# A graph-transformer block on one Trainium2 core: the ring of weights and the sums of their quarters move to the other side of on-chip memory

## The chip, the cores and the metric

The kernel runs on one core of one Trainium2 chip. The core has five engines that work at the same time, each through its own queue in order: TensorE (PE, the matmuls; its weight loads are listed apart as PEld), VectorE (DVE), ScalarE (ACT), GpSimd (POOL) and SyncE (SP), which here does nothing but issue DMA transfers. The metric is the device time of one launch in microseconds (us). Lower is better.

## The reference

The input x has 1250 nodes of 768 features; a graph of about 41,000 edges comes as two lists, src and dst. Cut to what matters here:

```python
xn = layernorm(x)
x = x + gnn(xn, edges) + mix(xn)
x = x + ffn(layernorm(x))

def gnn(xn, ...):            # two graph-attention layers: 4 heads, then 2 heads
    out1 = gat_conv(x_norm, src, dst, W1, ...)
    out2 = gat_conv(out1, src, dst, W2, ...)
    return concatenate([xn, out2]) @ Wu + bu

def mix(xn, ...):            # linear attention, 12 heads of 64
    q = elu(xn @ Wq + bq) + 1;  k = elu(xn @ Wk + bk) + 1;  v = xn @ Wv + bv
    kv = einsum(k, v);  z = 1 / einsum(q, k.sum())
    return (einsum(q, kv) * z) @ Wo + bo

def ffn(xl, ...):            # 8 experts of 384, the best 2 per node
    h = gelu(xl @ W1[e] + b1[e]);  y = h @ W2[e] + b2[e]
```

Everything is computed in 32-bit floats.

## The kernel before

The nodes are cut into ten tiles of 125 rows. The program has five stages, and each engine's instructions are put in order by a planner of the compiler, which lets later work go first where earlier work is blocked.

1. **Graph counts and features.** The edges become a 1250 x 1250 matrix of counts, `AT`, and a 0/1 matrix `mask`. The normalised, turned input stays in memory as `xnT`.
2. **Two layers of graph attention** (`attend`, lines 501 to 543). For each head ACT makes exponentials, DVE takes their maximum (line 541) and multiplies by the counts (line 542), and PE sums over neighbours (line 554 in the first layer, line 576 in the second).
3. **Keys and values** (lines 591 to 631). For each tile PE multiplies `xnT` by `Wk_sb` and `Wv_sb` (line 600). DVE makes keys of the one, ACT copies the other, PE multiplies them (line 614), and DVE adds the result to `kvacc` (line 620). The planner spreads these matmuls over the attention stage, where PE has time left; the last ones come after it. At the end DVE puts the bias of the values in and cuts the product to its heads (lines 628 and 630). Then PE turns `kvacc` (lines 673 and 674), and ACT copies it out as `kvT` and `ksum` (lines 675 and 676).
4. **Output of both branches.** `Wo_sb` is replaced by the product of `kvT` and `Wo` (lines 678 to 683: twelve matmuls of 384 columns, each of which the trace records as two). From then on queries, `Wo` and `Wu` are applied to pairs of tiles (`query(p)` and the loop from line 927). The big products, for Wq and for Wu, are done with seven products of quarters instead of eight (a scheme of Winograd's). For that, `quarters(W, T)` makes sums of the four quarters of a weight by four subtractions on DVE (lines 657 to 660): three results go to the tile T and one replaces a quarter of W. `pair(p)` makes the sums on the side of the input (lines 794 to 797). `product` is the matmul itself (line 802).
5. **Experts.** Nodes are gathered by expert with indirect DMAs on POOL (line 1029), turned, and put through the two layers of each expert (lines 1048 and 1060). The results are added to the output by indirect DMAs.

**Where tiles lie.** On-chip memory is handed out by pools stacked from two sides, left and right. Sizes below are bytes per partition. A pool that is opened after another was closed takes over its place, and the first instruction that writes there waits for the last one that used the old tile.

- On the left lie constants, then `xnT` (30,000; pool `big`), and in stages 1 to 3 the graph's tiles above it: `AT` 25,240, `mask` 12,500, `h2` 7,920 and `s1` 320. Above these come the attention's work tiles: `w` 3 x 5,000, `v` 2 x 5,000, `scr` 2,500, and the three rows `ss_row`, `up_row`, `dn_row` of 5,000 each. `graph.close()` (line 588) ends them after the second attention layer.
- On the right lie `kept` (31,680, holding among others `Wq_sb` and `kvT`), `kvacc` and its neighbours, and the pool `kp` of stage 3: `Wk_sb` 18,432, `Wv_sb` 18,432, `bk_b`, `ky`, `va` and `ke`, 50,712 in all. `kps.close()` (line 631) ends it.
- After that, the pool `mp` (`ksum`, `bq_b`) and the pool `wt` are opened on the right. `wt` is the ring of this case: four slots of 18,432 that hold in turn the sums of Wq's quarters (`aside[0]`), `Wo_sb`, `Wu_sb`, the sums of Wu's quarters (`aside[1]`), and later the weights of the experts, plus `Wu2_sb` (6,144) and `bu_b` (3,072). Behind them on the right lie the pool `fp` (expert biases, the gate's weights, `zero`, the broadcast biases `wb`) and, for stage 4 only, `rp` and `rl` (small tables and work tiles).
- `qp` (tiles `xt`, `qy`, `qe`, `qT` of stage 4) is opened on the left, above `xnT`. `first_half.close()` (line 1017) gives `xnT` up ahead of stage 5, and `sp`, the experts' work tiles, takes its place.

**Order of the DMA issues in the program** behind stage 3: `bq_b` (line 663), `Wo` and `Wu` (both by `load`, line 650), `Wu2_sb` (line 690), `fb`, `Wg_sb`, `bg_b` (lines 708 to 712), seven stores of zeros (lines 716 to 718), `bu_b` and `bo_b` (line 742), and then the tiles of x (line 933) and the weights of the experts (lines 699 to 704).

**What uses them.** `bq_b` is added to query products (line 819). `m1` and `w2` of lines 819 and 829 lie where `kvT` was, so they wait for line 682. `Wu2_sb` is read by the small product of line 748, whose result goes into `bu_b` (lines 743 and 750), which is added to every tile of x (line 934). `fb` is turned into `fb1T` (lines 774 and 775).

Of the kernel before, what the change touches and what calls it, by code (L numbers as in the profile page):

```python
# [27 lines left out]
F32 = mybir.dt.float32  # L28
# [10 lines left out]
N, D = 1250, 768  # L39
PT, NT = 125, 10  # L40
KC = D // 128
H1, C1, H2, C2 = 4, 192, 2, 96
# [27 lines left out]
def gps_block(ctx: ExitStack, tc: tile.TileContext, x, src, dst, norm_g, norm_b, W1, a_src1, a_dst1,  # L70
              b1, W2, a_src2, a_dst2, b2, Wu, bu, Wq, bq, Wk, bk, Wv, bv, Wo, bo, Wg, bg, fW1, fb1,
              fW2, fb2, out):
    nc = tc.nc
# [8 lines left out]
    const = ctx.enter_context(tc.tile_pool(name="const", bufs=1))  # L82
    small = ctx.enter_context(tc.tile_pool(name="small", bufs=3))
    dram = ctx.enter_context(tc.tile_pool(name="dram", bufs=1, space=bass.MemoryType.DRAM))
    first_half = ctx.enter_context(ExitStack())
    big = first_half.enter_context(tc.tile_pool(name="big", bufs=1))
    xr = x.rearrange("(t p) d -> p t d", p=PT)

    def token_rows(t):
# [550 lines left out]
    mp = ctx.enter_context(tc.tile_pool(name="mp", bufs=1, side="right"))  # L640
    ksum = mp.tile([PT, D], F32)
    bq_b = mp.tile([PT, D], F32)
    wt = ctx.enter_context(tc.tile_pool(name="wt", bufs=1, side="right"))
    q3 = KC // 2

    def weight():
# [31 lines left out]
    for c in range(KC):  # L678
# [7 lines left out]
    aside.append(weight())  # L686
    Ru = quarters(Wu_sb, aside[1].rearrange("p c f -> p (c f)")[:, :nt].rearrange(
        "p (c f) -> p c f", f=384))
    Wu2_sb = wt.tile([96, H2, D], F32)
    nc.sync.dma_start(Wu2_sb, Wu[D:].rearrange("(c p) f -> p c f", p=96))  # L690
    bu_b = wt.tile([PT, D], F32)


    fp = ctx.enter_context(tc.tile_pool(name="fp", bufs=1, side="right"))
# [32 lines left out]
    with ExitStack() as rs:  # L727
        rp = rs.enter_context(tc.tile_pool(name="rp", bufs=1, side="right"))
# [5 lines left out]
        def numbers(shape, pattern, base, mult, name, dt=F32):  # L734
# [2 lines left out]
                           allow_small_or_imprecise_dtypes=True)  # L737
            return t

        bo_b = qp.tile([PT, D], F32, name="xt")  # L740
        for t, a in ((bu_b, bu), (bo_b, bo)):
            nc.sync.dma_start(t, row_bcast(a, PT))
# [271 lines left out]


    mix.close()
    first_half.close()
    sp = ctx.enter_context(tc.tile_pool(name="sp", bufs=2))
    x_p = ctx.enter_context(tc.tile_pool(name="x_p", bufs=1, space=PSUM))
    h_p = ctx.enter_context(tc.tile_pool(name="h_p", bufs=2, space=PSUM))  # L1020
# [117 lines left out]
```

## Time and profile before

| | before |
|---|---|
| median of 3 runs | 1155.41 us (1152.61 to 1155.65) |
| the profiled execution, its own time | 1153.47 us |
| span of the profile | 1151.4 us |
| outside the span (1153.47 - 1151.4) | 2.07 us |
| PE busy | 1047.5 us (91%) |
| DVE busy | 706.8 us (61%) |
| ACT busy | 348.0 us (30%) |
| POOL busy | 74.3 us (6%) |
| mean granted PE clock | 0.973 of full speed |
| bytes moved by DMA | 79.76 MB, mean 69 GB/s |

The profile is one execution recorded by the hardware. Its views give the busy time of each engine, groups of instructions by line with what they waited for, the chain of work that ended last, and a timeline. Times within it count from the start of the span. A name such as `w` is the program's name for a tile with the number of its buffer left out: `w` with `in_L_mix_Wo_dram` is the ring's slot that receives Wo, and `kept` is the tile that holds `Wq_sb` and `kvT`. An ended wait is put down to the instruction whose signal came last. The granted clock is the share of PE's full clock that the chip let it have. PE's busy time counts modelled ends of matmuls, so it can hide waits of some tenths of a microsecond.

### The profile page before, as it was taken

What the parts mean: (1) busy time and instruction counts of PE and PEld (TensorE: products, weight loads), DVE (VectorE), ACT (ScalarE), POOL (GpSimd) and SP (SyncE); (2) the same over time, 40 slices, a digit from 0 to 9 for tenths busy, and PEclk for the clock granted to TensorE, in tenths of its full rate; (3) what the DMA queues carried; (4) which work ended last, traced back from release to release, by engine and by line L of the source; (5) the groups of instructions that cost most, each with busy time, mean ns of one, the idle gap of its engine ahead of it and who ended that gap; (6) DMA issues with size and microseconds to landing.
All of it is one profiled execution on the core that took longest, in us unless ns stands there. A gap on an engine that the chain in (4) does not pass through costs nothing.

```text
span 1151.4 us, 12014 instructions
## 1 busy us (share of the span) xinstructions
PE 1047.5 (91%) x4482; PEld 700.3 (61%) x4482; DVE 706.8 (61%) x1439; ACT 348.0 (30%) x522; POOL 74.3 (6%) x98
## 2 busy tenths in 40 slices
PE   2699998999999989988996999999999499999994
PEld 2596655579696969544553565666656356666653
DVE  7866667669696967769656757575755522222211
ACT  2141114464646454183832111111210011111111
POOL 1000000000000000000000000000000113222321
PEclk9999999999999999999997999999999689999997
DMA  5014000000000001100036001111144737787634
GB/s 160 28 46 173 14 28 1 1 1 1 1 1 1 1 0 44 40 1 1 14 83 217 9 28 54 41 41 41 41 141 136 241 80 190 216 208 213 124 56 57
DMA packets 35542, 79.76 MB, mean 69 GB/s; under 512 B 7006, under 2 KB 15536, under 8 KB 35468
## 3 DMA queue, kind: packets, MB, share of 16 engines
q1 hardware_dynamic: 29868, 59.06, 15.9%
q0 software_dynamic: 5600, 19.77, 8.5%
q8 instruction: 39, 0.64, 0.2%
q14 instruction: 35, 0.29, 0.1%
HBM read 60.48 MB, written 18.34 MB: 68 GB/s over the span
## 4 chain that ended last, share of the span: by engine, by line
PE 69%; DVE 21%; DMA 3%; issue 2%; ACT 2%; POOL 0%; DVEq 0%; POOLq 0%; ACTq 0%
PE s L802 18%; PE ph L1048 8%; PE mm L600 8%; PE py L1060 7%; PE mm L431 7%; DVE scr L521 6%; DVE w L541 5%; DVE w L542 5%; PE ag L554 3%; PE mm L861 2%; PE ag L576 2%; PE px L1032 2%; PE mm L406 2%; DMA out_dram<-ys,idx 1%; PE ec L351 1%
## 5 line engine op out<-in xcount | busy, mean ns | idle before, releaser
L554 PE MATMUL ag<-kept,w 125*125 125x198 f32 x800 | 137.4, 333 | 5.1 <-DVE w L542 4.9
L554 PEld LDWEIGHTS ag<-kept,w 125*125 125x125 f32 x800 | 133.5, 188 | 9.0 <-DVE w L542 9.0
L1048 PE MATMUL ph<-xsT,w 128*128 128x384 f32 (+1 forms) x324 | 100.7, 471 | 1.7 <-DVE xsT L1035 1.7
L1060 PE MATMUL py<-w,hT 128*128 128x384 f32 x300 | 100.6, 486 | 0.0
L431 PE MATMUL mm<-Wg,xnT 128*125 128x400 f32 x240 | 90.4, 514 | 1.1 <-DVE xnT L322 0.6
L541 DVE TENSOR_TENSOR w<-v,w 125x1250 f32<-125x1250 f32 x60 | 86.5, 1458 | 6.0 <-ACT w L539 5.3
L600 PE MATMUL mm<-Wv_sb,xnT 128*125 128x384 f32 x240 | 85.7, 489 | 4.8 <-DVE kvacc L620 4.8
L521 DVE CUSTOM_DVE_ANT_0 scr<-ss_row,mask 125x1250 bf16<-125x1250 f32 x60 | 87.5, 1459 | 0.5 <-ACT ss_row L512 0.2
L542 DVE SCALAR_TENSOR_TENSOR w<-w,AT 125x1250 f32<-125x1250 f32 x60 | 86.6, 1459 | 0.4
L1048 PEld LDWEIGHTS ph<-xsT,w 128*128 128x128 f32 x324 | 59.8, 194 | 41.3 <-DVE xsT L1035 2.3
L540 ACT ACTIVATE v<-dn_row,sl 125x1250 f32<-125x1250 f32 x60 | 79.4, 1335 | 17.3 <-DVE w L541 16.8
L600 PE MATMUL mm<-Wk_sb,xnT 128*125 128x384 f32 x240 | 84.4, 486 | 0.0
L802 PE MATMUL s<-w,qT 128*125 128x384 f32 x240 | 83.7, 490 | 0.0
L1035 DVE COPY xsT<-px 128x384 f32<-128x384 f32 x50 | 25.6, 553 | 86.7 <-PE px L1032 77.1
L1060 PEld LDWEIGHTS py<-w,hT 128*128 128x128 f32 x300 | 55.3, 190 | 33.9
L1063 DVE TENSOR_TENSOR ys<-py,wb 128x768 f32<-128x768 f32 x25 | 23.9, 958 | 72.4 <-PE py L1060 45.7
L600 PEld LDWEIGHTS mm<-Wv_sb,xnT 128*125 128x125 f32 x240 | 42.4, 187 | 31.1 <-DVE kvacc L620 7.0
L802 PE MATMUL s<-w 128*125 128x384 f32 x150 | 54.0, 494 | 7.5 <-DVE w L796 7.5
L802 PEld LDWEIGHTS s<-w,qT 128*125 128x125 f32 x240 | 43.3, 188 | 26.9 <-issue 0.2
L431 PEld LDWEIGHTS mm<-Wg,xnT 128*125 128x125 f32 x240 | 42.8, 191 | 26.8 <-issue 1.5
L539 ACT ACTIVATE w<-up_row,s 125x1250 f32<-125x1250 f32 x40 | 53.3, 1334 | 17.7 <-PE ag L554 17.5
L357 DVE TENSOR_TENSOR AT<-AT,ec 125x120 f32 x162 | 44.6, 275 | 19.9 <-PE ec L351 18.7
(296 smaller groups left out, 1458.8 us busy)
## 6 DMA issues: line engine op xcount, KB each, us to landing
w<-in_L_ffn_W_dram SPq DMA_DIRECT2D x18, 1152.0 KB
xt<-in_x_dram SPq DMA_DIRECT2D x20, 336.0 KB
wb<-in_L_ffn_b_dram SPq DMA_DIRECT2D x9, 384.0 KB
out_dram<-xt SPq DMA_DIRECT2D x10, 336.0 KB
xl_d<-xl SPq DMA_DIRECT2D x10, 336.0 KB
W_sb<-in_L_gnn_W_dram SPq DMA_DIRECT2D x1, 2304.0 KB
Wk_sb<-in_L_mix_Wk_dram SPq DMA_DIRECT2D x1, 2304.0 KB
Wv_sb<-in_L_mix_Wv_dram SPq DMA_DIRECT2D x1, 2304.0 KB
```

The costliest lines, as they stand in the source:

```text
L357: nc.vector.tensor_add(here, here, ec[:, g])
L431: nc.tensor.matmul(ps[:PT, :2 * (CG + 2)], xnT[:, c, t * PT:(t + 1) * PT], Wg1[:, c, 2 * k:2 * k + 2].rearrange("p h c -> p (h c)"), start ...
L521: nc.vector.tensor_tensor_reduce(scr, ss_row, mask[:, t], 1.0, 0.0, ALU.mult, ALU.max, top[:, t:t + 1])
L539: nc.scalar.activation(w, up_row, AF.Exp, bias=ss[:, st:st + 1])
L540: nc.scalar.activation(v, dn_row, AF.Exp, bias=sl[:, st:st + 1])
L541: nc.vector.tensor_tensor(w, v, w, op=ALU.max)
L542: nc.vector.scalar_tensor_tensor(w, w, 2.0, AT[:, st, :N], op0=ALU.min, op1=ALU.mult)
L554: nc.tensor.matmul(ag[:, t // 2, o:o + CG], w[:, t * PT:(t + 1) * PT], gw[:, st, hd], start=st == 0 and t % 2 == 0, stop=st == NT - 1, ski ...
L600: nc.tensor.matmul(ps[:PT, :384], xnT[:, c, t * PT:(t + 1) * PT], w[:, c, half], start=c == 0, stop=c == KC - 1)
L802: nc.tensor.matmul(ps, left[:, c], right[:, c], start=start and c == 0, stop=c == n - 1, skip_group_check=True)
L1048: nc.tensor.matmul(ph[:, :n * 128], w[0][:, o:o + 128], xT[:, c, :n * 128], start=c == 0, stop=c == KC - 1)
L1060: nc.tensor.matmul(py[:, k, :384], hT[:, f, j * 128:(j + 1) * 128], w[:, o:o + 384], start=f == 0, stop=f == FC - 1)
```

## The change

`wt` is opened on the left, above `xnT`, instead of on the right. It then covers 73,728 bytes that were the graph's 45,980, the attention's 27,500 of `w`, `v` and `scr`, and the first 248 of the row tiles. Since `qp` and later `sp` are stacked above `wt` on the left, `big` can't be closed ahead of stage 5 any more: it stays open to the end, and `first_half` goes. `Wu2_sb` and `bu_b` leave `wt` for `rp` on the right, and the load of `Wu2_sb` is written further down, behind the zeros and ahead of `bu_b`. With `wt` gone from the right, `fp`, `rp` and `rl` follow `mp` directly and lie where `kp` was.

```diff
-    first_half = ctx.enter_context(ExitStack())
-    big = first_half.enter_context(tc.tile_pool(name="big", bufs=1))
+    big = ctx.enter_context(tc.tile_pool(name="big", bufs=1))
...
     mp = ctx.enter_context(tc.tile_pool(name="mp", bufs=1, side="right"))
     ksum = mp.tile([PT, D], F32)
     bq_b = mp.tile([PT, D], F32)
-    wt = ctx.enter_context(tc.tile_pool(name="wt", bufs=1, side="right"))
+    wt = ctx.enter_context(tc.tile_pool(name="wt", bufs=1))
...
     Ru = quarters(Wu_sb, aside[1].rearrange("p c f -> p (c f)")[:, :nt].rearrange(
         "p (c f) -> p c f", f=384))
-    Wu2_sb = wt.tile([96, H2, D], F32)
-    nc.sync.dma_start(Wu2_sb, Wu[D:].rearrange("(c p) f -> p c f", p=96))
-    bu_b = wt.tile([PT, D], F32)
...
+        Wu2_sb = rp.tile([96, H2, D], F32)
+        nc.sync.dma_start(Wu2_sb, Wu[D:].rearrange("(c p) f -> p c f", p=96))
+        bu_b = rp.tile([PT, D], F32)
         bo_b = qp.tile([PT, D], F32, name="xt")
         for t, a in ((bu_b, bu), (bo_b, bo)):
             nc.sync.dma_start(t, row_bcast(a, PT))
...
     mix.close()
-    first_half.close()
     sp = ctx.enter_context(tc.tile_pool(name="sp", bufs=2))
```

No instruction that computes is added or removed.

## The prediction

> **What bounds the kernel now.** First the page's busy times and its 40 slices (28.8 us each).
>
> ```profile
> PE 1047.5 (91%) x4482; PEld 700.3 (61%) x4482; DVE 706.8 (61%) x1439; ACT 348.0 (30%) x522; POOL 74.3 (6%) x98
> ...
> PE   2699998999999989988996999999999499999994
> ...
> PEclk9999999999999999999997999999999689999997
> ```
>
> TensorE is the bound nearly everywhere. Behind the first stages it has two marked holes: slice 31 (a chain of small routing steps, which the change leaves alone) and around slice 21, where busy is 6 and the clock 7. The change touches the second. So I read it next, by stretches: length, then busy us of PE, PEld, DVE, ACT and POOL, granted clock, DMA share, GB/s.
>
> ```profile
> 589.30:594.20 4.90, 4.90 (x24) 2.97 (x23) 0.89 (x5) 1.77 (x4) 2.44 (x15) 1.00 0.55 158
> 594.20:602.20 8.00, 8.00 (x28) 4.48 (x26) 3.61 (x10) 0.52 (x1) 0.00 (x0) 1.00 0.78 195
> 602.20:605.50 3.30, 3.22 (x17) 2.25 (x17) 1.59 (x6) 1.08 (x6) 0.00 (x0) 1.00 0.04 15
> 605.50:609.00 3.50, 1.43 (x8) 0.96 (x8) 3.47 (x6) 2.12 (x12) 0.00 (x0) 1.00 0.38 92
> 609.00:617.66 8.66, 1.64 (x2) 0.49 (x3) 6.66 (x11) 0.00 (x0) 0.00 (x0) 0.57 1.00 372
> 617.66:625.00 7.34, 7.31 (x13) 3.70 (x14) 0.11 (x1) 2.51 (x6) 0.00 (x0) 0.58 0.85 294
> ```
>
> PE idles 2.07 us in the fourth line and 7.02 in the fifth, 9.09 together, and then works at little over half clock. The chain of work and SyncE's timeline say why.
>
> ```profile
> 594.42 7.74 PE mm L600 x24
> ...
> 603.87 0.57 DVE kvacc L620
> ...
> 606.22 11.33 DMA w<-in_L_mix_Wo_dram
> 617.69 11.62 PE mm L682 x24
> ```
>
> ```profile
> 568.51 0.35 SPq L625 DMA_DIRECT2D ky<-in_L_mix_bv_dram  x1
> 589.29 0.29 SPq L708 DMA_DIRECT2D fb<-in_L_ffn_b_dram  x1
> ...
> 605.89 0.28 SPq L663 DMA_DIRECT2D bq_b<-in_L_mix_bq_dram  x1
> 606.22 0.38 SPq L650 DMA_DIRECT2D w<-in_L_mix_Wo_dram  x1
> 606.64 0.54 SPq L650 DMA_DIRECT2D w<-in_L_gnn_Wu_dram  x1
> 607.23 5.32 SPq L690 DMA_DIRECT2D Wu_sb<-in_L_gnn_Wu_dram  x1
> ```
>
> Wo goes out only when stage 3 has ended, and the product of line 682 waits for it. SyncE's waits name both releasers:
>
> ```profile
> SPq L708 <- PE ag L576: 20.4, 1, 20.4
> SPq L663 <- DVE kvacc L628: 9.8, 1, 9.8
> ```
>
> `fb` now lies on the graph's ground and leaves as the last attention matmul ends, at 589.3. The loads on the ground of `kp` wait until 605.9. The planner passes later loads ahead of blocked earlier ones, as `fb` shows. The change swaps the two grounds.
>
> **The change part by part.**
>
> *Wo and Wu issue at about 589.4 instead of 606.2.* Wo's landing took 11.33 us beside Wu on the same queue, so Wo is there at 600.7. For both (4.72 MB): 1.5 us until bytes flow (the first full slice after the issue is 607 to 608), then 12.7 us at the 372 GB/s of the fifth line, so 603.6. The other end is the 195 GB/s of 594 to 602: 24.2 us, landing at 615.1. But that line holds small broadcast rows, which now go later; I take the first. What hides the loads: the last key and value matmuls, until 602.2.
>
> *The product of line 682* now waits for `kvT` instead. Its last copy in the trace ends at 608.45. So the product starts 9.2 us earlier at the latest (617.66 - 608.45).
>
> *The clock.* The product took 11.62 us; its last 12 records, at full clock, took 4.44 (624.78 to 629.22), so 24 take 8.9: 2.7 us gained. Line 802's pair in the fifth line took 1.64 where 0.81 is usual: 0.8 more. Here the Trainium skill ("TensorE: Matmul & The Clock Gate", The HAM clock gate) gives a smaller gain: half clock after about 3.4 us of idleness, full clock again after about 3.4 us of sustained work, so 1.7 us lost, a hole worth 9.09 + 1.7 = 10.8. The trace shows clock 0.50 from 611 to 623, 5 us and more after the product began: 3.5 lost, 12.6 in all. I use the trace. Against the change, the rule would charge again if the remaining gap reached 3.4 us; 605.5 to 609 has 2.07.
>
> *The remaining 2.07 us* end if PE has other work: the first query's quarter products 6, 7 and 2 (2.1 us each; four banks allow four until `m1`, which lies on `kvT`). They need the sums of Wq's quarters and of the input: 4 x 1.35 us and, for two pairs, 8 x 0.55 us on DVE, 9.8 us, now free to run from 589.3. DVE's idle time from 589.3 to 605.5 is 16.2 - 6.1 = 10.1 us, so they just fit. If that cover is gone they run behind `kvacc` as now and the gain is 12.6 - 2.07 = 10.5. I take 12.0, most of it filled.
>
> *What moves later.* `fb`, `Wg_sb`, `bg_b`, the zeros (589.29 to 593.93), `bo_b`, the first x tiles and `wb` now wait for `kp`. SyncE issues `bq_b` at 605.9, then 4.6 us of `fb` to zeros, then `Wu2_sb` at 610.9, `bu_b`, `bo_b` and x. With 3.6 us from issue to use (the x tile issued at 631.54, added at 635.13) `Wu2_sb` is there at 615. Its reader, line 748, follows the product, now ending at 617.4 (608.5 + 8.9): 2.4 us of slack. If the planner puts line 748 ahead of the product, PE stands until 615, 6.5 us. Line 774 (three transposes of `fb`, 0.23 us each) behind a landing at about 610: 0 to 2 us; I take nothing, since PE has queue entries with no such need. POOL's 15 small instructions (2.44 us) and DVE's two table steps serve routing at about 690; the slack is 80 us. `bq_b` needed 5.7 us from issue to line 668 beside Wo; its user, line 819, waits for the product anyway.
>
> *Edits at nothing.* `xnT` kept to the end, and `sp` on `qp`'s place: the first gather waits for `idx` (909.84 + 0.23), later than the last reader of `qT`; line 1012's last read of `rp`, under `sp`'s upper end, is at 911.8 against the gather's 911.06, so at most 0.7. The ring keeps four slots, so experts' loads keep their releases. From 640 to 880 PE idles 0.2 us; nothing there swallows a gain.
>
> **Sum.** 9.09 + 3.5 - 0.6 for imperfect filling = 12.0. Against the profiled execution: span 1151.4 - 12.0 = 1139.4, plus 2.07 outside = 1141.5. That execution (1153.47) lies 1.9 below the median of the runs, so against 1155.41 it is 1143.4. Changes under 0.3% (3.5 us) can't be told from none here.
>
> **Rivals.**
>
> *A new wait takes part of the place.* Line 748 ahead of the product (6.5), Wo and Wu at the slow rate (615.1 - 608.5 = 6.6), or DVE busy with new work when line 620 comes (one subtraction, 1.35). Gain 4 to 9; with 6.5 lost, 1149.9. For it: orders are the planner's, made from its own estimates. Against: 2.4 us of slack, and work to fill with.
>
> *The ring isn't free early.* Its 73,728 bytes take in 248 of the row tiles; were a tile of `kp` or anything living touched, or the release a joint one, Wo would go at 606.2 as now, `Wu2_sb` 4.6 us later than 607.2, and since its issue was held 5.3 us anyway, nothing moves: 1155.4. Against it: `fb`'s release at 589.3, and all those tiles belong to attention.
>
> *Slower: Wu's quarters block VectorE.* The four subtractions of line 657 to 660 on Wu (5.4 us) stood at 625 to 630.6, behind line 819. If the planner puts them ahead of line 620, everything behind, `kvacc`, `kvT`, the product, waits for Wu at L + 5.4 instead of 603.87, and PE goes cold (3.5). With L = 615.1 that costs 20.1: 1143.4 + 20.1 = 1163.5. It is worse than before by over 0.3% (15.5 lost) from L = 610.5 on. For it: Wu may now land while keys are unfinished. Against: L = 603.6 by the nearest row, and keys come first in the program.
>
> **How the numbers follow.** The full gain: 0.63, with its own range 1141 to 1146. A new wait: 0.18 (1146 to 1152). Not free: 0.07. Slower: 0.12. Faster by over 0.3% is the first two, 0.81; same 0.07; slower 0.12. The range leaves out the last two and little else: 1139.5 (all 12.6 of gain, 1142.8, and 3.3 for the scatter of the runs, which was 3.0) to 1152.5.
>
> **What would show it.** Right: Wo and Wu issued near 589.4, ahead of `bq_b`; no DMA piece ahead of line 682 in the chain of work; the product starting near 608.5 and lasting about 8.9; clock 1.00 from 600 to 640; the first sums of Wq's quarters on DVE ahead of line 620; the slice of PE at 8 or 9. Wrong: Wo still behind `bq_b`; line 748 or 774 waiting for a DMA; line 657 waiting for Wu with `kvacc` behind it; a changed order before 589, which nothing in the change asks for.

## The result and the profile after

| | before | after |
|---|---|---|
| median of the runs (6 and 6, on one chip) | 1155.04 us (1152.61 to 1156.33) | 1147.53 us (1145.15 to 1149.21) |
| ratio, 95% interval | | 0.9937 (0.9921 to 0.9952) |
| the profiled execution, its own time | 1153.47 us | 1146.65 us |
| span of the profile | 1151.4 us | 1144.8 us |
| mean granted PE clock | 0.973 | 0.976 |

The kernel is faster by 7.5 us between the medians, and by 7.3 (5.5 to 9.1) by the ratio. The prediction said 12.0, and so put the time 4.1 us too low, though the range of 1139.5 to 1152.5 holds it.

The listings follow those of the prediction, view by view. Most line numbers are one lower than before; between the old and the new place of `Wu2_sb`'s load they are four lower, and behind line 1016 two. The product of `kvT` and Wo is line 681, the reader of `Wu2_sb` line 747.

The 40 slices of the page (28.6 us each), PE's busy tenths and the granted clock:

```profile
PE   2699998999999989988999999999999499999994
...
PEclk9999999999999999989999999999999599999997
```

The hole around slice 21 is gone: PE shows 9 there and the clock is 9. The hole of the routing steps, slice 31, stays. The same stretches as in the prediction, with the same columns (length, busy us of PE, PEld, DVE, ACT and POOL, granted clock, DMA share, GB/s):

```profile
589.30:594.20 4.90, 4.90 (x20) 2.72 (x19) 3.36 (x5) 1.80 (x4) 0.00 (x0) 1.00 0.57 174
594.20:602.20 8.00, 8.00 (x30) 4.98 (x29) 7.13 (x17) 0.52 (x1) 0.00 (x0) 1.00 1.03 417
602.20:605.50 3.30, 3.30 (x17) 1.95 (x16) 2.60 (x6) 0.74 (x2) 0.00 (x0) 1.00 0.40 161
605.50:609.00 3.50, 3.48 (x19) 2.10 (x17) 1.76 (x9) 1.87 (x10) 2.15 (x15) 1.00 0.13 35
609.00:617.66 8.66, 8.66 (x26) 3.73 (x24) 6.90 (x8) 5.30 (x14) 0.27 (x2) 1.00 0.75 192
617.66:625.00 7.34, 5.29 (x17) 2.37 (x15) 0.00 (x0) 1.15 (x4) 0.00 (x0) 1.00 0.64 178
```

The transfers moved from the fifth line to the second (372 GB/s there before, 417 GB/s here now), under the last key and value matmuls. PE no longer idles in the fourth and fifth lines, and the clock is 1.00 throughout. The new thing is in the last line: PE is busy for 5.29 of 7.34 us, and DVE does nothing at all. SyncE's timeline (start, length, issue) says what came late:

```profile
590.26 0.37 SPq L649 DMA_DIRECT2D w<-in_L_mix_Wo_dram  x1
590.69 0.54 SPq L649 DMA_DIRECT2D w<-in_L_gnn_Wu_dram  x1
606.72 0.29 SPq L662 DMA_DIRECT2D bq_b<-in_L_mix_bq_dram  x1
...
609.92 0.52 SPq L713 DMA_DIRECT2D out_dram<-zero  x1
612.58 0.32 SPq L712 DMA_DIRECT2D xl_d<-zero  x1
...
613.90 0.45 SPq L737 DMA_DIRECT2D Wu_sb<-in_L_gnn_Wu_dram  x1
...
614.80 0.34 SPq L741 DMA_DIRECT2D xt<-in_L_mix_bo_dram  x1
```

Wo and Wu leave as attention ends and ahead of `bq_b`, as predicted. But between the fourth and the fifth store of zeros SyncE stands for 2.1 us, so `Wu2_sb` leaves at 613.90 and not at 610.9 (the other 0.8 us is `bq_b`'s own later issue). Its own row among the waits (us in total, times, longest) names the transfer that it stood for:

```profile
SPq L712 <- DMA bq_b<-in_L_mix_bq_dram: 2.1, 1, 2.1
```

The zeros have nothing to do with `bq_b`. But SyncE's transfers signal their landing on eight semaphores in turn (counters that an instruction can wait for; 101 to 108 in the trace's record), and where an issue waits on one of them, it is until the earlier transfer with the same semaphore has landed. The fifth store is the eighth issue behind `bq_b`, and both use 107. The same is seen behind another transfer: in the two versions below in which Wo leaves just ahead of these loads ("only Wo early" and "Wo late"), the store that stands is the eighth issue behind Wo.

What PE and DVE paid for it, from the waits of 600 to 630:

```profile
DVE bu_b L742 <- DMA xt<-in_L_mix_bo_dram: 9.3, 1, 9.3
...
PE mm L747 <- issue: 2.0, 1, 2.0
```

PE's timeline shows the place of the second row. It is put down to "issue". The trace's record of the semaphores shows what PE stood for: its queue waited at line 747 until 620.12 for the semaphore of `Wu2_sb`'s load, whose last signal came at 620.09, 6.19 us behind its issue:

```profile
609.27 8.86 PE L681 MATMUL mm<-w,kept 128*128 128x384 f32 x24
620.18 2.81 PE L747 MATMUL mm<-Wu_sb,col 96*125 96x384 f32 x8 [2.05 <-issue]
```

In the chain of work no transfer lies ahead of the product any more. The chain now comes through the broadcast rows instead:

```profile
606.72 5.84 DMA bq_b<-in_L_mix_bq_dram
...
614.80 11.13 DMA xt<-in_L_mix_bo_dram
...
626.02 0.97 DVE bu_b L742
```

**Where the time went.** Attention ends at other times in other executions (589.2 to 593.6), so I measure each profile from the start of its own last addition to `kvacc` (line 620 before, 619 after) to the first store of x in stage 4. That stretch took 79.87 us before and 69.81 after, 10.06 less. PE's busy time in it fell from 70.47 to 67.25 (the clock, 0.91 before and 1.00 after), and its idle time from 9.40 to 2.56. So 3.2 us came from the clock and 6.8 from the wait. Of the 2.56 us still idle, 2.05 are the wait of line 747.

Of these 10.06 us a part is given back later. The first gather of stage 5 now comes 2.95 us behind the start of `idx` (900.25 to 903.20) where it was 1.22 (909.84 to 911.06): 1.73 lost. The chains of work, of before and then of after:

```profile
909.93 0.14 DVE idx L979
...
910.68 0.39 PE g L1012
911.06 0.00 issue
911.06 4.53 DMA xg<-xl_d,idx
```

```profile
901.09 0.39 PE g L1011
901.50 0.29 DVE v_row L1012
...
901.83 0.39 PE g L1011
...
902.34 0.86 issue
903.20 4.05 DMA xg<-xl_d,idx
```

The first chain puts the gather down to the first transposition of the routing table, but that only ended at the same moment. By the record of the semaphores, the last wait of POOL's queue that ended in before was for `idx` (at 910.12, 0.28 us behind the start of `idx`), and in after for the second transposition (at 902.25, 2.00 us behind it). From there to the gather it is 0.94 or 0.95 us in all fourteen traces, so the "issue" of the second chain is no new cost: the release alone moved, by 1.72 us.

The whole way to the span's 6.6 us, in order of time: attention ended 0.97 us later (last section); the last `kvacc` came 0.16 sooner behind it; the stretch gave 10.06; the way from the first x store to `idx` 0.34; the gather lost 1.73; its way to the first expert product gave 0.53; and the experts, from there to the end of the span, took 229.90 us against 228.14, 1.76 lost. Together 6.6. The first of these lies ahead of the change. Whether the last belongs to it isn't shown: over the fourteen traces the experts took 227.1 to 229.9 us, after's being the longest.

### The profile page after: what moved, and what is told of

Read it like the earlier page. It is cut to its first block, busy times and chain, and to the rows that moved or that the text cites. A ratio compares the mean times of both kernels' runs of the same rounds, so it can differ in the third digit from the quotient of the medians.

```text
span 1144.8 us, 12035 instructions
## 1 busy us (share of the span) xinstructions
PE 1046.8 (91%) x4482; PEld 700.9 (61%) x4482; DVE 705.8 (62%) x1439; ACT 347.9 (30%) x522; POOL 74.2 (6%) x98
## 4 chain that ended last, share of the span: by engine, by line
PE 67%; DVE 23%; DMA 3%; issue 2%; ACT 2%; SPq 0%; POOL 0%; DVEq 0%; POOLq 0%; ACTq 0%
PE s L801 16%; PE ph L1046 9%; PE mm L599 8%; PE py L1058 7%; PE mm L430 7%; DVE scr L520 6%; DVE w L540 5%; DVE w L541 5%; PE ag L553 3%; PE mm L860 2%; PE ag L575 2%; PE mm L405 2%; PE px L1030 2%; PE ec L350 1%; PE g L875 1%
## 5 line engine op out<-in xcount | busy, mean ns | idle before, releaser
L599 PEld LDWEIGHTS mm<-Wk_sb,xnT 128*125 128x125 f32 x240 | 42.2, 187 | 23.5 <-issue 1.7
```

Source lines behind the costliest of these rows:

```text
L599: nc.tensor.matmul(ps[:PT, :384], xnT[:, c, t * PT:(t + 1) * PT], w[:, c, half], start=c == 0, stop=c == KC - 1)
```

## The experiments

**The theory (A):** Wo's early load is the whole gain. The hole is worth about 12.6 to 13 us, and it wasn't all got because `Wu2_sb`, `bu_b` and `bo_b` came late (PE's 2.05 us, and query products not done ahead), and because `sp` now lies over tiles of routing (1.7 us at the gather). **The rivals (B):** the gain comes from what else was moved (tables and expert biases on the ground of `kp`, zeros issued later); or the hole was never worth 12, and the waits shown cost nothing; or work put ahead of `kvacc` on DVE eats the gain, as the slower rival of the prediction had it.

Line numbers in the experiments differ from after's by a few. All runs were timed beside the kernel before on the same chip. As that kernel's own median differs between chips (1153.85 to 1155.04), I compare ratios; a gain in us is (1 - ratio) times the median of before beside it.

### `Wu2_sb` and `bu_b` back in the ring's pool

The load is issued with Wo's, early; nothing else differs from after.

```diff
+    Wu2_sb = wt.tile([96, H2, D], F32)
+    nc.sync.dma_start(Wu2_sb, Wu[D:].rearrange("(c p) f -> p c f", p=96))
+    bu_b = wt.tile([PT, D], F32)
...
-        Wu2_sb = rp.tile([96, H2, D], F32)
-        nc.sync.dma_start(Wu2_sb, Wu[D:].rearrange("(c p) f -> p c f", p=96))
-        bu_b = rp.tile([PT, D], F32)
```

> The changed kernel with Wu2_sb and bu_b put back into the ring's pool (now on the left), and Wu2_sb's load written where it was. Theory A, small loads made late (the 2.05 us before the product with Wu2_sb come from its late issue): that wait goes, Wu2_sb issues near 590, 1145.5 us; VectorE still waits for bo_b. Theory B, the missing gain lies elsewhere (order, end of the kernel): 1147.5 us as the changed kernel.

Measured: 1143.46 us, ratio 0.9905 (0.9890 to 0.9919), a gain of 11.0 us: theory A, and lower than its 1145.5. PE's timeline, as above for after:

```profile
611.08 8.86 PE L681 MATMUL mm<-w,kept 128*128 128x384 f32 x24
619.86 2.84 PE L747 MATMUL mm<-Wu_sb,col 96*125 96x384 f32 x8
```

Line 747 follows the product with no wait. The stretch from the last `kvacc` to the first x store is 66.97 us with 0.23 idle: 12.90 less than before, which is what the prediction had said of the hole (9.09 + 3.5 = 12.6). So the late load cost after 2.84 us. 2.05 of them are PE's wait and 0.28 other idle time. The last 0.5 is busy time, and not products put off: the traces have the same 224 matmuls in both stretches. `bo_b` is still issued late here (615.83), and DVE stands 5.0 us for it without PE's losing time: that wait of DVE alone is covered.

### All three early: `Wu2_sb`, `bu_b` and `bo_b` in a pool above the ring

To make room, two work tiles of the routing, `gt` and `eq`, have one buffer instead of two.

```diff
+    bs = ExitStack()
+    bp = bs.enter_context(tc.tile_pool(name="bp", bufs=1))
+    Wu2_sb = bp.tile([96, H2, D], F32)
+    nc.sync.dma_start(Wu2_sb, Wu[D:].rearrange("(c p) f -> p c f", p=96))
+    bu_b = bp.tile([PT, D], F32)
+    bo_b = bp.tile([PT, D], F32)
+    for t, a in ((bu_b, bu), (bo_b, bo)):
+        nc.sync.dma_start(t, row_bcast(a, PT))
...
-            gt = rl.tile([PT, NE, NE], F32, name="gt")
+            gt = rl.tile([PT, NE, NE], F32, name="gt", bufs=1)
...
     mix.close()
+    bs.close()
```

> The changed kernel with Wu2_sb, bu_b and bo_b in a pool of their own on the left, right above the ring, all loaded ahead of fb (two small routing tiles have one buffer instead of two to make room). Theory A: both the 2.05 us of TensorE and the 9.3 us that VectorE stood at the addition of bo_b go; TensorE then keeps the lead that the early query products gave it: 1143.5 to 1144.5 us. Theory B: 1147.5 us.

Measured: 1142.98 us, ratio 0.9893 (0.9879 to 0.9908), a gain of 12.4 us. That is theory A's time, but the chain of work shows a cost that the expectation didn't have:

```profile
586.48 10.77 DMA bo_b<-in_L_mix_bo_dram
597.34 0.06 DVE bu_b L744
...
600.95 0.55 DVE kvacc L619
```

With its load free to go early, the planner put the bias addition (line 744) ahead of the sums of quarters and of `kvacc` on DVE, and the second of the two broadcast rows took 10.8 us to land. DVE stood 6.4 us for it. In the 10 us ahead of the last `kvacc` PE was busy for 8.92, where before and after have 10.00. The stretch behind is the shortest of all, 66.33 us, and the gather came 1.22 us behind `idx`, probably since `rp` is smaller now and `sp` begins where these loads had lain.

### The gather's tiles in a pool of their own

`xT`, `gates` and `xg` get a pool that is opened ahead of `sp` and so takes the lowest ground, where `qp` was.

```diff
     mix.close()
+    gp = ctx.enter_context(tc.tile_pool(name="gp", bufs=2))
     sp = ctx.enter_context(tc.tile_pool(name="sp", bufs=2))
...
-        xT = sp.tile([128, KC, FIX * 128], F32, name="xsT")
-        gates = sp.tile([128, FIX], F32, name="gates")
+        xT = gp.tile([128, KC, FIX * 128], F32, name="xsT")
+        gates = gp.tile([128, FIX], F32, name="gates")
...
-            xg = sp.tile([128, D + NE], F32, name="xg", bufs=3)
+            xg = gp.tile([128, D + NE], F32, name="xg", bufs=3)
```

> The changed kernel with the gathered rows, their turned form and the gates in a pool of their own that is opened ahead of the rest of the experts' tiles, so that it lies on qp's place alone and touches neither rp nor rl. Theory A, a pool waits as a whole for every pool that it overlaps: the first gather goes about 1.0 us after idx as in the kernel before, not 2.7; 1146 us. Theory B, the gather's delay has another cause: still 2.7 us after idx, 1147.5 us.

Measured: 1143.15 us, ratio 0.9909 (0.9893 to 0.9924), a gain of 10.5 us. The gather in the chain of work:

```profile
901.63 4.20 DMA xg<-xl_d,idx
```

The gather leaves 1.23 us behind `idx`, and POOL's queue waited for `idx` alone (until 900.68), both as before. So theory A holds: what after lost there was due to the ground of `sp`. (PE's wait at line 747 was 0.6 us in this execution; the stretch, 69.21 us, is hardly shorter than after's.) The timed gain over after is 3.2 us, more than the 1.7 of this wait, but the intervals of the two ratios overlap (0.9924 and 0.9921), and 1.7 lies within them. In this trace the experts took 227.1 us where after's took 229.9.

### Only Wo early: Wu, `Wu2_sb`, `bu_b` and the rest of the ring on the right

Wo gets a pool on the left; the ring has three slots on the right, and every fourth expert uses Wo's.

```diff
-    wt = ctx.enter_context(tc.tile_pool(name="wt", bufs=1))
+    wt = ctx.enter_context(tc.tile_pool(name="wt", bufs=1, side="right"))
+    wo_p = ctx.enter_context(tc.tile_pool(name="wo_p", bufs=1))
...
-    Wo_sb = weight()
+    Wo_sb = wo_p.tile([128, KC, D], F32, name="w", bufs=1)
```

> The kernel before with Wo's slot alone on the graph's ground on the left (three slots, Wu2_sb and bu_b stay on the right; xnT is kept to the end). The prediction's step, Wo's landing is the hole: the product of kvT and Wo starts right behind kvT, clock stays at 1.00, only the 2.07 us of filling are missing, and Wu2_sb goes out right behind bq_b and Wu: 1143 to 1146 us. Rival, the early sums of quarters and the early Wu carry the gain: above 1150 us.

Measured: 1147.46 us, ratio 0.9939 (0.9922 to 0.9955), a gain of 7.0 us. This is nearly all that after has, and the rival (above 1150 us) is out. The product starts 4.28 us behind the last `kvacc`, as early as in after (4.59). But the time is above the 1143 to 1146 expected, so Wo's early load alone is not the best version. Wu's load stands at 609.8 on the queue now, and `Wu2_sb` behind it (the chain of work):

```profile
609.78 0.39 SPq L651
...
610.22 14.89 DMA Wu_sb<-in_L_gnn_Wu_dram
```

It lands at 625.1. By then PE has done other query products for 3.2 us and idled 1.3. Another 1.1 us PE idles ahead of the product, at the transpositions of `kvacc`. The stretch is 69.90 us, no better than after's.

### The sums of Wq and Wo on the left, Wu and its sums on the right

The ring's four slots as two pools of two, `Wu2_sb` and `bu_b` in the right one, and the gather's tiles in a pool of their own.

```diff
+    wl = ctx.enter_context(tc.tile_pool(name="wl", bufs=1))
...
-    Wo_sb = weight()
+    Wo_sb = weight(wl)
...
-    Wu_sb = weight()
+    Wu_sb = weight(wt)
```

> The kernel before with the ring split: two slots on the graph's ground (the sums of Wq's quarters and Wo), two on the right (Wu and the sums of its quarters) with Wu2_sb and bu_b, and the gather's pool. Theory A, only Wo and Wq's sums need to be early; then fb, the zeros and bo_b stay early too. Wu2_sb goes out behind Wu at 608 and lands behind it, so the product with Wu2_sb waits up to 4 us as with Wo alone: ratio 0.991 to 0.993. Rival, nothing early is lost and it is the best of all: below 0.989.

Measured: 1143.83 us, ratio 0.9905 (0.9884 to 0.9926), a gain of 11.0 us. `Wu2_sb` lands late as in the version above (14.20 us after its issue at 610.54), and PE idles 0.6 us for it; the stretch is 69.20 us, and the gather comes 1.23 us behind `idx`. Two early slots thus do as well as four, with the gather's pool in both (11.0 and 10.5 us).

### The ring on the left, but Wo late

The reverse: everything where after has it, but Wo alone on the right, on ground that stays taken until `kps.close()`. The ring has three slots; with it smaller, `qp` lies lower, and `bo_b` and the first tile of x leave early too (589.33 and 590.09).

```diff
+    wo_p = ctx.enter_context(tc.tile_pool(name="wo_p", bufs=1, side="right"))
...
-    Wo_sb = weight()
+    Wo_sb = wo_p.tile([128, KC, D], F32, name="w", bufs=1)
```

> The changed kernel with Wo's slot alone put on the right, on the ground of the keys' and values' weights; sums and Wu stay early (and qp, now 18,432 bytes lower, no longer reaches that ground, so bo_b and the first x tile are early). Theory of the prediction, Wo's landing makes the hole: Wo issues near 607, lands by 614 to 615 since Wu no longer shares the queue, the product starts there and not at 609.3, with a hole or query products in it: 1149 to 1153 us. Rival, early sums of quarters fill the hole as well, so Wo need not be early: 1147.5 us or less.

Measured: 1154.04 us, ratio 0.9995 (0.9982 to 1.0008). The gain is gone. SyncE's timeline and, from the waits, PE's:

```profile
589.66 0.37 SPq L651 DMA_DIRECT2D w<-in_L_gnn_Wu_dram  x1
...
607.90 0.26 SPq L664 DMA_DIRECT2D bq_b<-in_L_mix_bq_dram  x1
608.22 0.39 SPq L651 DMA_DIRECT2D w<-in_L_mix_Wo_dram  x1
```

```profile
PE mm L683 <- issue: 7.9, 1, 7.9
```

Wu leaves early, Wo late, and PE idles 7.9 us ahead of the product, which starts at 619.72. The last signal of Wo's landing came at 619.63, so it is Wo that the "issue" hides. This is the clearest verdict of the study: Wo's early load is the gain, and neither Wu's nor the moved tables. It also corrects a size. I had expected Wo to land sooner with Wu out of its way; it still took 11.4 us, from 608.22 to 619.63, as long as beside Wu before (11.33). This is the likely reason why the time is above the 1149 to 1153 expected.

### Only the tables moved

Against before: the ring stays on the right; `Wu2_sb` and `bu_b` leave it for `rp`, with the load behind the zeros.

```diff
-    Wu2_sb = wt.tile([96, H2, D], F32)
-    nc.sync.dma_start(Wu2_sb, Wu[D:].rearrange("(c p) f -> p c f", p=96))
-    bu_b = wt.tile([PT, D], F32)
...
+        Wu2_sb = rp.tile([96, H2, D], F32)
+        nc.sync.dma_start(Wu2_sb, Wu[D:].rearrange("(c p) f -> p c f", p=96))
+        bu_b = rp.tile([PT, D], F32)
```

> The kernel before with only Wu2_sb and bu_b moved to rp and their load behind the zeros; the ring stays on the right. Theory A (they hurt the changed kernel only because the product of line 682 no longer hides them): 1155 us, within 2 of the kernel before. Rival, moving them costs by itself: 1157 to 1159 us.

Measured: 1156.57 us, ratio 1.0023 (1.0014 to 1.0032): 2.7 us slower than before, between theory A (within 2) and the rival (1157 or more). So this half of the change gains nothing, and the chain of work shows a mechanism close to the slower rival of the prediction:

```profile
599.17 10.60 DMA xt<-in_L_mix_bo_dram
609.80 0.96 DVE bu_b L743
610.75 0.48 DVE kvacc L620
```

The bias addition stands ahead of the last `kvacc` on DVE and waits for `bo_b`, whose load took 10.60 us. What blocked DVE was a broadcast row and not Wu's quarters, but the place is the one that the rival named: in the 10 us ahead of the last `kvacc` PE was busy for 8.72. That is 1.3 of the 2.7 us; the rest isn't explained.

### Broadcast rows over 128 partitions

In after, `bq_b`, `bu_b` and `bo_b` are loaded over 128 partitions instead of 125; only 125 are used.

```diff
-    bq_b = mp.tile([PT, D], F32)
+    bq_b = mp.tile([128, D], F32)
...
-    nc.sync.dma_start(bq_b, row_bcast(bq, PT))
+    nc.sync.dma_start(bq_b, row_bcast(bq, 128))
+    bq_b = bq_b[:PT]
...
-            nc.sync.dma_start(t, row_bcast(a, PT))
+            nc.sync.dma_start(t, row_bcast(a, 128))
+        bu_b, bo_b = bu_b[:PT], bo_b[:PT]
```

> The changed kernel with its three broadcast rows bq_b, bu_b and bo_b loaded into 128 partitions instead of 125 (the last three rows are not used). Theory A, a row sent to 125 partitions is slow because it can be spread over few of the 16 DMA engines, and 128 spreads over all: bq_b lands in 2.5 to 3.5 us instead of 5.84, SyncE is no longer held 2.1 us among the zeros, bo_b lands in under 6 us instead of 11.13, the 2.05 us ahead of the product with Wu2_sb go: 1144.5 us. Theory B, the landing time follows the bytes and what else is on the queue: landings within 15% of the changed kernel's, 1147.5 us.

The Trainium skill ("DMA: Bandwidth & Descriptors", Why a DMA increments its semaphore by 16 and not by 1) says that a transfer is dealt to the largest number of DMA engines, up to 16, that divides the slowest dimension on both of its sides; 128 partitions give 16. By that rule 125 rows, on 125 partitions, give 5. One microsecond each in which `bq_b` is moved (stretches, columns as above; DMA share is the last but one), of after and then of this version:

```profile
608.00:609.00 1.00, 1.00 (x8) 0.77 (x6) 0.00 (x0) 0.69 (x5) 1.00 (x11) 1.00 0.30 106
```

```profile
609.00:610.00 1.00, 1.00 (x8) 0.68 (x7) 0.21 (x2) 0.73 (x4) 1.00 (x8) 1.00 0.74 184
```

0.30 is about 5 of 16 engines (0.31), and 0.74 is more than 5 can give. Other small loads run in the same microseconds, so the shares alone would not decide it. The record of the semaphores does: when `bq_b` lands, five signals come in after (612.37 to 612.57) and sixteen in this version (610.73 to 611.76). The trace agrees with the page. The row landed in 3.6 us instead of 5.84, and `bo_b` in 6.5 instead of 11.13, both a little above what theory A expected. SyncE's stand behind `bq_b` disappears from its waits, line 749 (after's 747) follows the product without a wait, and the stretch is 67.19 us. The time, however, is 1145.74 us, ratio 0.9933 (0.9918 to 0.9949), a gain of 7.7 us, between the two theories and not to be told from after's 7.3. The profiled execution, at 1142.94 us, was the lowest of six, so it isn't typical of its kernel. The mechanism is seen in the trace; that it saves time is not shown by this run.

### The same in before

```diff
-    bq_b = mp.tile([PT, D], F32)
+    bq_b = mp.tile([128, D], F32)
...
-    nc.sync.dma_start(bq_b, row_bcast(bq, PT))
+    nc.sync.dma_start(bq_b, row_bcast(bq, 128))
+    bq_b = bq_b[:PT]
```

(and `bu_b` and `bo_b` likewise)

> The kernel before with nothing changed but bq_b, bu_b and bo_b in 128 partitions. Theory A, the 11.33 us of Wo's landing were in good part bq_b, which sat ahead of Wo on five of the sixteen engines: Wo lands in 8 to 9.5 us, the hole of TensorE shrinks by 2 to 3 us, ratio 0.997 to 0.998. Rival, Wo took that long because Wu shares the queue: landing at 11 us or more, ratio 1.000.

Measured: 1153.62 us, ratio 0.9998 (0.9986 to 1.0010). The chain of work:

```profile
606.97 10.58 DMA w<-in_L_mix_Wo_dram
...
617.68 10.48 PE mm L683 x24
```

Wo took 10.58 us instead of 11.33: 0.75 less and not 2 to 3, and nothing of it can be seen in the time. The record of the semaphores shows what the narrow row does to Wo. Sixteen signals tell of Wo's landing. In before, eleven of them came by 616.09 and five between 617.07 and 617.55; here they come without such a gap, from 615.83 to 617.54. With Wo late and behind the narrow row, eleven came by 618.08 and five between 619.37 and 619.63. So five of the sixteen shares were held up by about 1.5 us where the row in five shares went ahead. The rest of what Wo took there without Wu isn't explained, and I leave it open.

### Two and three repairs together

`Wu2_sb` and `bu_b` in the ring, and the gather's pool (the first and third diffs):

> Both single repairs together on the changed kernel: Wu2_sb and bu_b in the ring's pool, and the gather's tiles in a pool of their own. If the two lost stretches are separate (2.0 to 2.8 us ahead of line 682's end to the first x, 1.7 at the first gather) their gains add: the product with Wu2_sb follows without a wait, the first gather goes 1.2 us after idx: 1141 to 1142 us. If what the two single runs gained was the chance of the last stage, no more than either alone: 1143.3 us.

Measured: 1143.75 us, ratio 0.9915 (0.9898 to 0.9932), a gain of 9.8 us. In its profile both waits are gone (stretch 66.97 us, gather 1.23 us behind `idx`), but the time is no better than with either repair alone, and above the 1141 to 1142 that the sum of both would give.

These two, and the wide rows:

> The two repairs of the changed kernel together (Wu2_sb and bu_b in the ring's pool, the gather's pool) and the broadcast rows in 128 partitions. Theory A: VectorE's 4.5 us at bo_b shrink to under 1; TensorE had work then anyway, so at most 1 us more than without the wide rows: ratio to the kernel before 0.990 to 0.991. Rival, the gains of the wide rows and of the early Wu2_sb are separate and add: 0.988 to 0.989.

Measured: 1143.05 us, ratio 0.9903 (0.9881 to 0.9924), a gain of 11.2 us; stretch 66.96 us. The ratio is theory A's. VectorE's wait for `bo_b` shrank to 2.8 us, not to under 1.

All three loads early in a pool above the ring (and so one buffer for `gt` and `eq`), wide rows, and the gather's pool:

> The changed kernel with Wu2_sb and both biases in a pool right above the ring and loaded early, the rows in 128 partitions, and the gather's pool. In the run with the early biases in 125 partitions VectorE stood at their addition ahead of the last additions to kvacc, 2.5 us. Theory A (slow rows): that wait goes, since the rows land in 4 to 5 us: stretch from the last addition to kvacc to the first store of x 66.3 us or less, ratio 0.988 to 0.9895. Rival (the order alone does it): VectorE still stands there, ratio 0.990.

Measured: 1142.04 us, ratio 0.9889 (0.9868 to 0.9911), a gain of 12.8 us. The ratio is theory A's, and the stretch (66.58 us) misses its 66.3 by a little. It is the lowest time of all. Its interval does not overlap after's; nor do those of "`Wu2_sb` in the ring" and "three loads early", from which it can't be told apart. The stretches of its trace:

```profile
606.00:610.00 4.00, 4.00 (x20) 2.62 (x19) 3.61 (x12) 1.29 (x5) 0.35 (x2) 1.00 0.01 4
610.00:618.00 8.00, 8.00 (x30) 3.93 (x27) 6.51 (x9) 4.81 (x15) 2.09 (x14) 1.00 0.68 189
618.00:626.00 8.00, 8.00 (x24) 3.59 (x23) 3.12 (x6) 2.83 (x8) 0.00 (x0) 1.00 0.52 161
```

PE has no hole left. The wait that the version with three early loads had for `bo_b` (6.4 us) is down to 0.8 us, as the wide row lands in 5.1 us and not in 10.8.

### All runs against the traces

"Stretch" is from the last `kvacc` to the first x store, "gather" from the start of `idx` to the first gather, each in the profiled execution. "By the trace" adds what both differ from before's 79.87 and 1.22; what happens outside the two isn't in it.

| version | stretch | gather | gain by the trace | gain measured (95%) |
|---|---|---|---|---|
| after | 69.81 | 2.95 | 8.3 | 7.3 (5.5 to 9.1) |
| `Wu2_sb` in the ring | 66.97 | 2.94 | 11.2 | 11.0 (9.4 to 12.7) |
| three loads early | 66.33 | 1.22 | 13.5 | 12.4 (10.6 to 14.0) |
| gather's pool | 69.21 | 1.23 | 10.7 | 10.5 (8.8 to 12.4) |
| only Wo early | 69.90 | 2.94 | 8.3 | 7.0 (5.2 to 9.0) |
| two slots left, two right | 69.20 | 1.23 | 10.7 | 11.0 (8.5 to 13.4) |
| ring left, Wo late | 75.72 | 2.94 | 2.4 | 0.6 (-0.9 to 2.1) |
| tables only | 79.51 | 1.23 | 0.4 | -2.7 (-3.7 to -1.6) |
| wide rows | 67.19 | 2.95 | 11.0 | 7.7 (5.9 to 9.5) |
| before, wide rows | 78.01 | 1.23 | 1.9 | 0.2 (-1.2 to 1.6) |
| ring and gather | 66.97 | 1.23 | 12.9 | 9.8 (7.8 to 11.8) |
| wide, ring and gather | 66.96 | 1.23 | 12.9 | 11.2 (8.8 to 13.7) |
| wide, three early, gather | 66.58 | 1.23 | 13.3 | 12.8 (10.3 to 15.2) |

Eight of the thirteen sums lie within the interval. The other five are above it: by 0.3 us (ring left with Wo late, and before with wide rows), 1.1 (ring and gather), 1.5 (wide rows) and 2.0 (tables only, where 1.3 us of PE's time are lost ahead of the stretch). In all but one the measured gain is the smaller. So the two waits account for the size of after's gain, but repairs that the traces show added up are not shown to add up in the time.

## Why the prediction was right or wrong

**The place and the mechanism: right.** Wo and Wu issued at 590.26 and 590.69 (predicted 589.4, with attention's end at 589.3 and not at 590.2). With Wo late, all of the gain is gone.

**The product: right.** It was predicted 9.2 us earlier and came 9.4 earlier, measured from each trace's own end of attention (617.69 - 589.29 = 28.40 us before, 609.27 - 590.26 = 19.01 after). It was to last 8.9 us and lasted 8.86.

**The clock: right, and the trace's figure was the better one.** 3.5 us were taken from the trace, and 1.7, an estimate, would have followed from the page of the Trainium skill that the prediction names ("TensorE: Matmul & The Clock Gate", The HAM clock gate); PE's busy time over the stretch fell by 3.2 in after, and by 3.7 in the version with `Wu2_sb` in the ring.

**The landing of Wo and Wu: right as to side.** The transfers filled 594 to 602 at 417 GB/s, near the 372 GB/s that I took and twice the 195 of the other end, and no one waited for them. Their last signals came at 598.43 and 604.06 (600.7 and 603.6 predicted). Wo thus took 8.17 us beside Wu with nothing ahead of it, where the 11.33 that I took over from before had `bq_b` ahead.

**The filling of the remaining hole: right, and then undone.** The sums of Wq's quarters stood at 590.3 to 597.3 on DVE, ahead of the last `kvacc`, and PE idled 0.02 us of the 3.50 from 605.5 to 609 (2.07 before).

**`Wu2_sb`: the step that failed first.** "SyncE issues `bq_b` at 605.9, then 4.6 us of `fb` to zeros, then `Wu2_sb` at 610.9 ... is there at 615 ... 2.4 us of slack." Two terms were too small. The 4.6 us counted the issues and took the queue to be free between them; SyncE stood 2.1 us for `bq_b`'s landing in the middle of the zeros, and the issue came at 613.90. And 4.1 us were taken for the landing, which took 6.19; why isn't shown. So `Wu2_sb` was there 5.1 us later than predicted (620.09 for 615) and the product ended 0.7 later (618.13 for 617.4): 2.4 us of slack became a wait of 2.05, to which the stand gave less than half. With the load issued early, the stretch is 2.84 us shorter. I had named this as a rival's wait ("a new wait takes part of the place") but with another cause, the planner's order.

**The gather: the step that failed second.** "At most 0.7" set the last read of `rp` (911.8) against the gather's start in before (911.06). But the gather's wait had ended at 910.12 there, 0.94 us ahead of its start. Set against that, the read is 1.7 later, and 1.73 us is what was lost. The version with the gather's own pool has 1.23 again.

**The sum.** 12.0 was the value of a hole closed with nothing new in its place: the version without the wait of line 747 measured 12.90 us in the stretch. Less 2.84 and 1.73 this is 8.3, and 7.5 was measured. The difference of 0.8 is within the interval. In the one trace of after it is larger, since attention (0.97) and the experts (1.76) took longer there.

**The rivals.** "A new wait takes part of the place" is what came, by its mechanism and by its number: 1147.53 us lies in its 1146 to 1152, to which I gave 0.18, and not in the 1141 to 1146 of the full gain, to which I gave 0.63. The stated range holds the time only because it took in this rival. "The ring isn't free early" is out: it was free at 590.26. "VectorE blocked by Wu's quarters" didn't happen in after, since the quarters of Wu stood at 609.1 to 615.7, behind `kvacc`. Its mechanism, DVE standing for a transfer with `kvacc` behind, is real in this kernel: it cost in "tables only" and, less, in "three loads early", both times by the bias addition. In after `bo_b` left only at 614.80, and the bias addition stood behind `kvacc`.

## What to carry to other kernels

When a load is moved to an earlier place, follow every transfer that changes places with it to its reader, and count the queue's own waits and not only its issues: here an issue stood until the transfer eight places ahead had landed, and 2.1 us of such waiting for one small broadcast row, with a landing 2.1 us slower than assumed, turned 2.4 us of slack into 2.05 us of idle TensorE. A tile that becomes free early also lets the planner put its reader early on an engine that works in order, so a load can be too early for the work behind its reader. And the ground that a pool is given decides when its first writer starts, at the far end of the kernel too.

## What was not expected of the hardware

**A row broadcast to 125 partitions is slow.** 384,000 bytes (125 rows of 3,072) took 5.84 us in after, with five signals of landing; a row with another one ahead of it took 10.6 to 11.1. With 128 partitions and sixteen signals it was 3.6, and 6.5 behind another row. Wo, 2.36 MB, took 11.33 beside Wu and behind such a row, and 8.17 beside Wu with nothing ahead.

**The same gap of TensorE costs clock in one execution and none in another.** Some 400 us ahead of the change, PE idles 2.8 us for a layer norm, in every trace with the same instructions. Stretches of before and then of after, with the columns as above:

```profile
192.00:196.00 4.00, 3.77 (x32) 2.61 (x31) 2.75 (x8) 3.65 (x7) 0.00 (x0) 1.00 0.00 0
```

```profile
192.00:196.00 4.00, 3.91 (x19) 2.50 (x18) 1.99 (x6) 2.93 (x6) 0.00 (x0) 0.57 0.00 0
```

Before went on at full clock, after at 0.57, and from 191 to 217 it lost 1.2 us. The gap before work was 2.78 us in the one and 2.77 in the other. Of the fourteen traces, three show no loss there (before, before with wide rows, and the ring on the left with Wo late), five a loss of about 1.1 us and six of about 2. The Trainium skill ("TensorE: Matmul & The Clock Gate", The HAM clock gate) charges from about 3.4 us of idleness; here 2.8 were enough, in some executions. One trace of each kernel can't tell whether it is chance or goes with the kernel. Before's own executions, though, had mean granted clocks from 0.958 to 0.977, so its clock does differ between executions of one program. In the traces half clock always lasts a multiple of 3.41 us (3.41 to 30.7, save for the one cut off by the end), so how the gap lies to these steps may matter; that is not tested. The loss is of the size of what is missing between the traces' gains and the measured ones, and I leave it open.
